# Other places for side work between the matrix products of a four-layer graph network, and one swap in the order of its block products

## The chip, the cores and the metric

The kernel runs on one core of one Trainium2 chip. The metric is the device time of one execution in microseconds, the median of several runs. A profiled execution of the same kernel gives the trace that the views below are taken from; its span runs from the first to the last instruction of the core.

## The reference

There are 3327 nodes with 256 features each, and one symmetric matrix `adj` of 3327 x 3327, in float32. Each of four layers normalises x over its features, takes the positive part and adds its result to x:

```python
h = relu(layernorm(x));  x = x + adj @ (h @ W.T + b)                      # layer 0
h = relu(layernorm(x));  A1 = top_k(tanh(adj*adj) where adj > 0, 700)     # layer 1
                         x = x + relu(A1 @ (tanh(h @ Wp + bp) @ Wg) + bg)
h = relu(layernorm(x));  A2 = D^-1/2 (adj + I) D^-1/2                     # layer 2
                         x = x + relu(A2 @ (h @ W.T))
h = relu(layernorm(x))                                                    # layer 3
R = rows of (adj + I) divided by their sums;  Xf = Xa = h;  Z = 0
for n in (0, 1):
    A = top_p_attention(Xa)      # softmax((Xa W1' W2')(Xa W3')'), the largest to 0.9 of the mass
    Xf = R @ Xf;  Xa = A @ Xa;  Z += Xf @ U1[n].T + Xa @ U2[n].T
x = x + layernorm(h + Z)
```

Every layer is therefore a product of a 3327 x 3327 matrix with 256 columns; layer 3 has two of them (R and A) in each of two steps, and the second step's A depends on the first step's result.

## The kernel before

The nodes are padded to 27 tiles of 128 rows. Rows are worked on in pairs, m and m + 13 (H = 13 pairs, T = 27 tiles). A pair's block product, seen as 2 x 2 blocks, is done with seven products of half size instead of eight: sums of blocks of `adj` (s1, s2, s4 and one in place, made by VectorE in `Feed.adding`, L553 to L556) and sums of the right side (`ts`). All of TensorE's work is float32 transposes and matmuls.

**Layers 0 to 2.** `products` loops over the pairs p = 0 to 12. `Product.steps` yields a number for each matmul call, called a step here; there are 7 x 13 = 91 for a pair, in three column cuts (`CUTS`, of 5, 4 and 4 blocks). In each cut the seven products come in the order of `PLACE`: 1, 2, 5, 4, 7, 3, 6. Product 5 uses s1 and product 3 uses s4, so that in the first cut s1 is first read at step 10 and s4 at step 25. When a product is finished (`result`, L619 to L630, and a `finish` function), the pair becomes a `Pair` of the next layer, which is normalised by VectorE (L404, and L460 for the last layer) and has a list of stages that TensorE must do: `turn` (transposes, L416, evicted by ScalarE at L420), `hidden` (L478, layer 1 only, followed by a tanh) and a last one: `second` (layer 1), `scaled` (layer 2) or `keys` (layer 3). The stages of pair p are put between the steps of the product of pair p + 1: the tables `WHERE`, `WHERE_KEYS` and `WHERE_FIRST` give the step numbers by how many stages there are. In layer 0 the first two pairs run together (`begin`), so that pair 2 carries the stages of two pairs, six in all. In layers 1 and 2 the first cut of the product of pair 1 is done early, inside that of pair 0 (`early`), and pair 0's stages are hooked into products 1 and 2 by a line of their own (`hooks, carried`). In layer 2 `counted` adds a small matmul (`pc`, L734) that sums the number of positive entries of a row pair over the partitions; its sum comes from VectorE (L724 to L729), and `counts` is read at the end of the kernel.

**Layer 3, first step.** `propagate_first` does R's product in 26 runs: pair p has two phases, each with products of 13 matmuls, in the order of `PHASES` (`FIRST_PHASES` for pair 0). `PLACE3` gives the accumulator bank of every product: 1, 2, 4 and 5 go to bank 0, 6, 7 and 3 to bank 1. After phase 0 (for pair 0 after phase 1) `half` copies bank 0 to SBUF on ScalarE (L1302), and there are two such accumulator buffers (`ps_acc`). A slab of 13 blocks of `adj` or of its stored sums is loaded through SP's queue when its product begins, and POOL adds the unit matrix to some (L1262). Between its matmuls the run does the attention of other rows: logits (L1061, four chunks: 0, 1 and 3 in `ps_row`, two buffers; 2 in both buffers of `ps_tr`), their exponentials on ScalarE (L1086), a threshold search (`search_steps`: one pass Relu at L1119 and one Sign at L1124 on ScalarE, the others on VectorE, ending with L1164 which keeps the large entries of e), and then the product of row m (`Rows`: transposes L202, evictions L205, matmuls L213). A finished row becomes, by `AttentionOfFirstStep`, a node of the second step: `turn`, `node` (L269 in one buffer of `ps_row`, evicted by L277 and L281, with a DMA L282) and `values` (L1344, also in `ps_row`). In the 19 interleaved rows these stand at fixed places of the run, which are in 27ths of its length: turn 3, node 9, logits of row m + 3 at 10, values 18, and the first transposes of row m + 1 at 20.

**Layer 3, second step.** The same search with the new keys; its first row (i = 0) also holds the last `turn` and `sums` of the first step's propagation (`of_next`).

TensorE's order is the program's: layer 3 is under a manual schedule in which TensorE keeps its order and the queues of the other engines are filled by a scheduler, with `high_priority` for evictions. [...] Several buffers are pairs, so that a matmul can wait for an eviction two uses before.

Of the kernel before, what the change touches and what calls it, by code (L numbers as in the profile page):

```python
# [47 lines left out]
def kernel(  # L48
# [94 lines left out]
    def run(steps, at=None):  # L143

        for k in steps:
            for what in (at or {}).get(k, ()):
                what()

    def merged(*plans):
        out = {}  # L150
        for p in plans:
            for k, v in p.items():
                out.setdefault(k, []).extend(v)
        return out
# [137 lines left out]
    def layers_0_to_2(again):  # L292
# [79 lines left out]
        def combine_nodes(rhs, a, b):  # L372
            run(combining_nodes(rhs, a, b))
# [258 lines left out]

        WHERE = {2: (60, 84), 3: (48, 61, 76), 6: (12, 22, 34, 46, 58, 70)}
        WHERE_KEYS = (81, 90)
        WHERE_FIRST = {2: (58, 86), 3: (52, 66, 83)}

        def products(layer, width, rhs, feed, finish, before, pair_after, following=None, counted=None, begin=None):

            todo = before.stages if before else []
            n, early = 0, []
            for p in range(H):
                if begin and p < 2:
                    if p == 0:
                        n, firsts = begin(lambda p: Product(layer, p, rhs, feed, width))
                    prod = firsts[p]
                else:  # L650
                    prod = early[0] if early and p == 1 else Product(layer, p, rhs, feed, width)
                    if p == 0:
                        for c in range(len(CUTS) if not before else 0):
                            combine_nodes(rhs, *CUTS[c])
                        if before:
                            combine_nodes(rhs, CUTS[2][0], H - 1)
                    at = WHERE_KEYS if layer == 2 and p else (WHERE if p else WHERE_FIRST).get(len(todo), ())
                    hooks = dict(zip(at, todo))
                    if early and p == 1:
                        hooks, carried = {86: todo[0]}, {14: todo[1]}  # L660
                    elif early and p == 2:
                        hooks.update(carried)
                    if counted:
                        hooks[62] = functools.partial(counted, p)

                    def steps(prod, c, a, b, past=0):
                        for at in prod.steps(c, a, b):
                            if at + past in hooks:
                                hooks[at + past]()

                    for c, (a, b) in enumerate(CUTS):
                        if early and p == 1 and not c:
                            n += 1
                            continue
                        feed.upto(n)
                        if p == 0 and before and b == H:
                            steps(prod, c, a, b - 1)
                            early.append(Product(layer, 1, rhs, feed, width))
                            steps(early[0], 0, *CUTS[0], 12 * 7)
                            combine_nodes(rhs, b - 1, b)  # L680
                            steps(prod, c, b - 1, b, 1000)
                        else:
                            steps(prod, c, a, b)
                        n += 1
                        if p == H - 1 and c and following:
                            combine_nodes(following, *CUTS[c - 1])
                    feed.upto(n)
                hold[:] = []
                if early and p == 0:
                    feed.upto(n + 1)  # L690
                    hold.append(feed.added)
                y, p3 = prod.result(feed.added if begin and p == 0 else None)
                x2 = feed.x2.pop(p)
                with tc.high_priority() if p == H - 1 else nullcontext():
                    finish(p, x2, y, p3)
                    pair = pair_after(p, x2)
                todo = pair.stages if p or not begin else []
                if begin and p == 1:
                    todo = first.stages + todo
                first = pair  # L700
            return pair
# [215 lines left out]
        else:  # L917
# [10 lines left out]
            with tc.tile_pool(name="tk", bufs=2) as tk, tc.tile_pool(name="tk1", bufs=1) as tk1:  # L928
# [9 lines left out]
                for p in range(H):  # L938
                    y = work.tile([P, 2, D], F32, tag="y", name=f"y1b_{p}")
                    for i in range(2):  # L940
                        m = p + i * H
# [54 lines left out]
    def layer_3_in(again, tag, big, ep, w3, sm3, h3, kT0, ksum0, left):  # L996
# [225 lines left out]

        added = []
        PHASES = (1, 2, 5, 4), (6, 7, 3)
        FIRST_PHASES = (1, 2, 3), (5, 7, 6, 4)
        PLACE3 = {2: (0, 0), 1: (0, 1), 4: (0, 2), 5: (0, 3), 6: (1, 0), 7: (1, 1), 3: (1, 2)}

        def combining(h, ts, a, b):
# [12 lines left out]
        class PropagatedPair:  # L1241
# [28 lines left out]
            def steps(self, phase):  # L1270

                first = self.p == 0
                ns = (FIRST_PHASES if first else PHASES)[phase]
                units = [(n, k) for n in ns for k in range(H)]
# [329 lines left out]
        with tc.manual_schedule(engines=PE_ALONE):  # L1604
# [10 lines left out]
            def passes(finder):  # L1615


                if finder is None:
                    return {}
                next(finder)  # L1620

                def one_more():
                    with tc.issue_after(last_turned[-1].ins):
                        next(finder, None)

                return {0: [one_more], 2: [one_more], 3: [lambda: next(finder, None)]}

            def passes_apart(step, finder):


                if finder is None:
                    return {}, {}

                first = passes(finder)[0]

                def second():
                    with tc.issue_after((last_copied if step == 0 else last_scaled)[-1].ins):
                        next(finder, None)
                    next(finder, None)

                return {0: first}, {4 if step == 0 else 0: [second]}
# [3 lines left out]
            def propagate_first(n, at):  # L1645

                p, phase = divmod(n, 2)
                pair = pairs.setdefault(p, PropagatedPair(0, p, h3, ts))
                units = H * len((PHASES if p else FIRST_PHASES)[phase])
                run(pair.steps(phase), {int(k * units // T): v for k, v in at.items()})  # L1650
# [42 lines left out]
            for i in range(EARLY):  # L1693
                plan = {}
                if props:
                    p = props.pop(0)
# [20 lines left out]
            rows = Rows(0, h3)  # L1717
# [3 lines left out]
            for m in range(T):  # L1721
                interleaved = m + AHEAD < T and m not in APART
                plan, later = passes_apart(0, finder) if interleaved else (passes(finder), {})
                plan = merged(plan, left_over)
                if props:
                    p = props.pop(0)
                    at = (3, 5, 6) if m == 0 else (2 if interleaved else 1, 3, 5)
                    plan = merged(plan, dict(zip(at, ([p.scale], [p.turn], [p.sums]))))
                if m + AHEAD < T and not interleaved:
                    plan = merged(plan, {4: [lambda: next(prepare(0, m + AHEAD, kT0))]})  # L1730
                alone = not interleaved and m != T - 3 and m + 1 < T
                if alone:
                    plan = merged(plan, {5: [lambda: rows.begin(m + 1)]})
                a = AttentionOfFirstStep(m, rows.finish(m, plan), dens.pop(m), f"{m}")
                if interleaved:
                    left_over = {}
                    steps = prepare(0, m + AHEAD, kT0)
                    after = {3: [a.turn], 9: [a.node], 18: [a.values], 20: [lambda: rows.begin(m + 1)]}
                    propagate_first(next(propagated), merged(whole_run(steps, 10), after, later))
                elif m == T - 3:  # L1740
                    left_over = {}
                    after = {1: [a.turn], 4: [a.node], 8: [a.values], 22: [lambda: rows.begin(m + 1)]}
                    propagate_first(T - LATE, after)
                elif alone:
                    left_over = {0: [a.turn], 1: [a.node], 3: [a.values]}
                finder = find(0, m + AHEAD, st0) if m + AHEAD < T else None
# [45 lines left out]
        with tc.manual_schedule(engines=PE_ALONE):  # L1792
# [3 lines left out]
            p = props.pop(0)  # L1796
            propagate_first(T - 2, merged(whole_run(steps_of_second, 8), {9: [lambda: p.scale(last_exp)], 16: [p.turn], 20: [p.sums]}))
            p = props.pop(0)
# [21 lines left out]
            rows = Rows(1, vs)  # L1820
# [3 lines left out]
            for i, m in enumerate(ORDER):  # L1824
                ahead = ORDER[i + AHEAD] if i + AHEAD < T else None
                plan, later = passes_apart(1, finder) if ahead else (passes(finder), {})
                if i == 0:
                    p, q = props
                    plan = merged({4: plan[0]}, {5: [p.scale, q.scale]})
                    of_next = {2: [p.turn], 5: [q.turn], 10: [p.sums], 14: [q.sums]}  # L1830
                acc = rows.finish(m, plan)
                ys[m] = attention_of_second_step(m, acc, dens.pop(m), f"{m}")
                plan = whole_run(prepare(1, ahead, kT1), 7) if ahead else {}
# [18 lines left out]
                p, phase = m % H, m // H  # L1852
# [111 lines left out]
```

## Time and profile before

| What | us |
|---|---|
| Median of 3 runs (lowest, highest) | 2517.3 (2516.82, 2521.48) |
| Profiled execution | 2517.92 |
| Its span | 2516.1 |
| TensorE busy, weight loads busy | 2486.4, 2254.9 |
| VectorE busy | 2095.5 |
| ScalarE busy | 1086.3 |
| POOL busy | 296.9 |

The mean clock that was granted to TensorE is 0.997 of full speed. PE are TensorE's matmuls, PEld its weight loads, DVE is VectorE, ACT ScalarE, POOL GpSimd and SP the engine that issues most transfers. A float32 matmul shows as two records. In a row of the timeline there stand start, duration, engine, line, operation, output and inputs, shape and number of records, and in brackets the idle time before it and the engine and line that ended it. A view of waits sums these brackets by the waiting line and the one waited for. The timeline puts neighbouring records of one line in one row, so a row's duration is from its first start to its last end.

### The profile page before, as it was taken

What the parts mean: (1) busy time and instruction counts of PE and PEld (TensorE: products, weight loads), DVE (VectorE), ACT (ScalarE), POOL (GpSimd) and SP (SyncE); (2) the same over time, 40 slices, a digit from 0 to 9 for tenths busy, and PEclk for the clock granted to TensorE, in tenths of its full rate; (3) what the DMA queues carried; (4) which work ended last, traced back from release to release, by engine and by line L of the source; (5) the groups of instructions that cost most, each with busy time, mean ns of one, the idle gap of its engine ahead of it and who ended that gap; (6) DMA issues with size and microseconds to landing.
All of it is one profiled execution on the core that took longest, in us unless ns stands there. A gap on an engine that the chain in (4) does not pass through costs nothing. (4 is left out here: it accounts for less than half of the span.)

```text
span 2516.1 us, 47844 instructions
## 1 busy us (share of the span) xinstructions
PE 2486.4 (99%) x17967; PEld 2254.9 (90%) x17967; DVE 2095.5 (83%) x5536; ACT 1086.3 (43%) x2158; POOL 296.9 (12%) x462
## 2 busy tenths in 40 slices
PE   9999999999999999999999999999999999999998
PEld 8999999999999998888888888888888888888887
DVE  7777788888887778788879797884999999999995
ACT  3011033443111115565656565663655655555551
POOL 2000010000000001000000100000121122222221
PEclk9999999999999999999999999999999999999999
DMA  6777765555698867223132323133533343344333
GB/s 200 226 227 240 224 196 172 177 174 182 224 311 299 275 213 233 96 81 108 57 112 88 108 85 105 55 108 104 172 118 112 108 138 119 109 134 141 117 117 105
DMA packets 181774, 388.28 MB, mean 154 GB/s; under 512 B 19741, under 2 KB 78746, under 8 KB 181530
## 3 DMA queue, kind: packets, MB, share of 16 engines
q1 hardware_dynamic: 153210, 364.31, 44.4%
q10 hardware_dynamic: 28320, 20.80, 2.6%
q8 instruction: 143, 2.34, 0.4%
q14 instruction: 101, 0.83, 0.1%
HBM read 315.44 MB, written 67.89 MB: 152 GB/s over the span
## 5 line engine op out<-in xcount | busy, mean ns | idle before, releaser
L205 ACT COPY eT_a<-pt_a 128x512 f32<-128x512 f32 (+1 forms) x364 | 196.7, 555 | 375.9 <-PE pt_a L202 372.6
L213 PE MATMUL a<-h3a,eT_a 128*128 128x256 f32 x1352 | 322.5, 381 | 0.2 <-ACT eT_a L205 0.2
L213 PE MATMUL a<-vs,eT_a 128*128 128x256 f32 x1352 | 320.2, 381 | 0.2 <-ACT eT_a L205 0.2
L1148 DVE MAX8 cand_a<-w 128x8 f32<-128x128 f32 x1352 | 288.4, 278 | 4.3
L213 PEld LDWEIGHTS a<-h3a,eT_a 128*128 128x128 f32 x1352 | 244.0, 189 | 32.8 <-issue 1.9
L213 PEld LDWEIGHTS a<-vs,eT_a 128*128 128x128 f32 x1352 | 244.8, 190 | 30.3 <-ACT eT_a L205 0.7
L603 PE MATMUL acc_a<-tsa,s_a 128*128 128x128 f32 (+1 forms) x2028 | 269.9, 275 | 0.0
L603 PE MATMUL acc_a<-tsa,a_a 128*128 128x128 f32 x2028 | 251.2, 275 | 0.0
L603 PE MATMUL acc_a<-rhs,a_a 128*128 128x128 f32 (+1 forms) x2028 | 250.3, 277 | 0.0
L603 PEld LDWEIGHTS acc_a<-tsa,s_a 128*128 128x128 f32 x2028 | 249.1, 192 | 0.6
L603 PEld LDWEIGHTS acc_a<-tsa,a_a 128*128 128x128 f32 x2028 | 239.5, 192 | 0.6
L603 PEld LDWEIGHTS acc_a<-rhs,a_a 128*128 128x128 f32 x2028 | 238.6, 193 | 0.6
L1144 DVE SCALAR_TENSOR_TENSOR w<-e_a,t_a 128x896 f32<-128x896 f32 x208 | 226.1, 1087 | 3.0
L1262 POOL TENSOR_TENSOR slab3a<-slab3a,ident 128x128 f32<-128x128 f32 x100 | 115.0, 1150 | 900.1 <-DMA slab3a<-in_adj_t_dram 383.7
L1086 ACT ACTIVATE e_a<-pl_a 128x1024 f32<-128x1024 f32 x260 | 184.7, 728 | 42.2 <-PE pl_a L1061 28.4
L202 PE MATMUL pt_a<-ident,e_a 128*128 128x128 f32 x1352 | 198.7, 273 | 0.6 <-DVE e_a L1164 0.3
L1135 DVE SCALAR_TENSOR_TENSOR w<-e_a,t_a 128x3328 uint8<-128x3328 f32 x52 | 191.8, 3689 | 4.3
L1164 DVE SCALAR_TENSOR_TENSOR e_a<-e_a,all_least 128x3328 f32<-128x3328 f32 x52 | 192.1, 3695 | 1.8
L202 PEld LDWEIGHTS pt_a<-ident,e_a 128*128 128x128 f32 x1352 | 165.5, 141 | 29.9 <-ACT eT_a L205 2.6
L420 ACT ACTIVATE xT_a<-pt_a 128x512 f32<-128x512 f32 x52 | 30.9, 595 | 355.7 <-PE pt_a L416 321.4
L753 ACT ACTIVATE a_a<-a_a 128x640 f32<-128x640 f32 (+1 forms) x156 | 101.5, 666 | 161.7 <-DVE a_a L751 129.1
L1293 PE MATMUL f0a<-tsa,slab3a 128*128 128x128 f32 x1352 | 166.2, 276 | 0.0
(265 smaller groups left out, 4213.0 us busy)
## 6 DMA issues: line engine op xcount, KB each, us to landing
slab3a<-s_dram SPq DMA_DIRECT2D x100, 832.0 KB, 4.4
a_a<-in_adj_t_dram SPq DMA_DIRECT2D x312, 256.0 KB, 4.0
slab3a<-in_adj_t_dram SPq DMA_DIRECT2D x79, 832.0 KB, 4.5
a_a<-in_adj_t_dram SPq DMA_DIRECT2D x156, 320.0 KB, 3.8
s_dram<-s_a SPq DMA_DIRECT2D x78, 256.0 KB, 4.9
s_dram<-s_a SPq DMA_DIRECT2D x39, 320.0 KB, 4.3
x_dram<-x_a ACTq DMA_DIRECT2D x39, 256.0 KB, 4.1
s_dram<-a_a SPq DMA_DIRECT2D x26, 256.0 KB, 5.1
```

Of the source, the lines that this page charges most:

```text
L202: nc.tensor.transpose(pt[:, j, :], e[:, k * P : (k + 1) * P], ident)
L205: last_turned.append(nc.scalar.copy(eT[:, : len(blocks), :], pt[:, : len(blocks), :]))
L213: nc.tensor.matmul(acc[:, :width], ready[g][:, j, :], rhs[:, k, :], start=(k == 0), stop=(k == T - 1))
L603: nc.tensor.matmul(self.acc[:, g, at : at + wide], quads[n][:, k - CUTS[c][0], :], t, start=(k == 0 and n in (1, 4)), stop=(k == H - 1 and ...
L753: nc.scalar.activation(a, a, AF.Tanh)
L1086: last_exp.append(nc.scalar.activation(dst, src, AF.Exp, accum_out=parts[:, c : c + 1]))
L1135: nc.vector.scalar_tensor_tensor(junk, e, t, e, ALU.is_lt, ALU.mult, accum_out=got)
L1144: nc.vector.scalar_tensor_tensor(w[:, : (b - a) * P], eg, t, eg, ALU.is_lt, ALU.mult, accum_out=below[:, g : g + 1])
L1148: nc.vector.max(cand[:, 8 * k : 8 * k + 8], w[:, (k - a) * P : (k - a + 1) * P])
L1164: nc.vector.scalar_tensor_tensor(e, e, least, e, ALU.is_ge, ALU.mult, accum_out=st["kept"][:, m : m + 1])
L1262: added.append(nc.gpsimd.tensor_tensor(x[:, p, :], x[:, p, :], ident, ALU.add))
L1293: nc.tensor.matmul(self.accs[bank][:, c * P : (c + 1) * P], a, self.right(n, k), start=start, stop=last.get(bank) == (n, k), skip_group_ch ...
```

## The change

There are six edits, all of them to places and orders; no operation is added or removed.

1. Layer 0: the six stages in pair 2 stand at steps 20, 30, 40, 50, 60, 72 instead of 12, 22, 34, 46, 58, 70.
2. Layer 1: in pair 0's product, which holds the last pair of layer 0, the stages `hidden` and `second` stand at 70 and 84 instead of 66 and 83.
3. Layers 1 and 2: pair 0's `turn` moves from step 86 of product 1 to step 10 of product 2, and its next stage from 14 to 34 there. The text of the change calls it the second pair's, since it stood in the second pair's product.
4. Layer 2: the count of pair 1 moves from step 62 of product 1 to step 22 of product 2; those of other pairs stay at 62.
5. Layer 3: in the second phase of pair 0 product 4 comes ahead of product 6, with its slab's load.
6. Layer 3: in the interleaved rows `node` moves from 9 to 15, and so behind the logits at 10; and in the first row of the second step the four items of `of_next` move from 2, 5, 10, 14 to 4, 8, 11, 15.

```diff
-        WHERE = {2: (60, 84), 3: (48, 61, 76), 6: (12, 22, 34, 46, 58, 70)}
+        WHERE = {2: (60, 84), 3: (48, 61, 76), 6: (20, 30, 40, 50, 60, 72)}
         WHERE_KEYS = (81, 90)
-        WHERE_FIRST = {2: (58, 86), 3: (52, 66, 83)}
+        WHERE_FIRST = {2: (58, 86), 3: (52, 70, 84)}
...
                     if early and p == 1:
-                        hooks, carried = {86: todo[0]}, {14: todo[1]}
+                        hooks, carried = {}, {10: todo[0], 34: todo[1]}
                     elif early and p == 2:
                         hooks.update(carried)
-                    if counted:
+                    if counted and early and p == 1:
+                        carried[22] = functools.partial(counted, p)
+                    elif counted:
                         hooks[62] = functools.partial(counted, p)
...
         PHASES = (1, 2, 5, 4), (6, 7, 3)
-        FIRST_PHASES = (1, 2, 3), (5, 7, 6, 4)
+        FIRST_PHASES = (1, 2, 3), (5, 7, 4, 6)
...
-                    after = {3: [a.turn], 9: [a.node], 18: [a.values], 20: [lambda: rows.begin(m + 1)]}
+                    after = {3: [a.turn], 15: [a.node], 18: [a.values], 20: [lambda: rows.begin(m + 1)]}
...
-                    of_next = {2: [p.turn], 5: [q.turn], 10: [p.sums], 14: [q.sums]}
+                    of_next = {4: [p.turn], 8: [q.turn], 11: [p.sums], 15: [q.sums]}
```

## The prediction

> **What bounds the kernel now.** I read the busy shares first, then TensorE's waits, then the timeline around each wait that the change touches. The chain that ended last shows only the kernel's tail (0% for every line), so it says nothing here.
>
> ```profile
> PE 2486.4 (99%) x17967; PEld 2254.9 (90%) x17967; DVE 2095.5 (83%) x5536; ACT 1086.3 (43%) x2158; POOL 296.9 (12%) x462
> ```
>
> TensorE is the bound: only what it idles, or runs at half clock, can be won. Its waits (releaser: us in total, times, longest):
>
> ```profile
> PE pt_a L416 <- DVE xn_a L404: 5.4, 4, 2.1
> PE pt_a L416 <- DVE h3a L460: 2.9, 1, 2.9
> PE f0a L1293 <- ACT xf_0a L1302: 2.4, 1, 2.4
> ...
> PE pc L734 <- DVE pos L729: 1.5, 1, 1.5
> PE pl_a L1061 <- ACT qT L281: 1.3, 4, 0.3
> PE hid_a L478 <- ACT xT_a L420: 0.8, 1, 0.8
> ```
>
> These six are what the change aims at. Around them in the timeline of TensorE and VectorE (start, duration, engine, line; the bracket is the idle time before):
>
> ```profile
> 84.68 0.76 PE L416 MATMUL pt_a<-ident,xn_a 128*128 128x128 f32 x4 [1.45 <-DVE xn_a L404]
> ...
> 400.77 1.11 PE L416 MATMUL pt_a<-ident,xn_a 128*128 128x128 f32 x4 [2.09 <-DVE xn_a L404]
> 401.68 1.91 PE L603 MATMUL acc_a<-tsa,s_a 128*128 128x128 f32 x8
> ...
> 401.56 0.82 DVE L553 TENSOR_TENSOR s_a<-a_a,a_a 128x640 f32<-128x640 f32 x1
> ...
> 691.27 0.18 PE L734 MATMUL pc<-ones,pos 128*128 128x1 bf16 x1 [1.49 <-DVE pos L729]
> ...
> 699.36 0.42 DVE L460 TENSOR_SCALAR h3a<-h3a 128x512 f32<-128x512 f32 x1
> 699.84 0.66 PE L416 MATMUL pt_a<-ident,h3a 128*128 128x128 f32 x4 [2.92 <-DVE h3a L460]
> ...
> 701.28 3.96 PE L603 MATMUL acc_a<-rhs,a_a 128*128 128x128 f32 x20
> ...
> 971.51 1.83 PE L1293 MATMUL f0a<-h3a,slab3a 128*128 128x128 f32 x14 [2.41 <-ACT xf_0a L1302]
> ...
> 998.09 3.67 DVE L1164 SCALAR_TENSOR_TENSOR e_a<-e_a,all_least 128x3328 f32<-128x3328 f32 x1
> ...
> 1002.21 1.04 PE L202 MATMUL pt_a<-ident,e_a 128*128 128x128 f32 x8
> ...
> 1437.07 1.13 PE L1061 MATMUL pl_a<-kT_0a,qT 64*128 64x512 f32 x4
> 1438.54 2.27 PE L1061 MATMUL pl_a<-kT_0a,qT 64*128 64x512 f32 x12 [0.34 <-ACT qT L281]
> ```
>
> ```profile
> 967.86:1001.77 33.91, 31.50 (x243) 27.58 (x242) 33.51 (x90) 22.70 (x48) 6.79 (x8) 1.00 0.61 206
> ```
>
> Undisturbed, 128-wide matmul records start every 0.112 us and a product step (two records) takes 0.223 us; 20 records of L603 take 2.40 us. The row at 701.28 takes 3.96: the clock granted after the two longest waits was half for 3.41 us, costing some 1.7 us each time, though the column reads 0.997 over the span. The last row gives, for 33.9 us, the busy time of PE, PEld, DVE, ACT and POOL: VectorE is full (33.51) just before e_0 is finished by L1164.
>
> [...] waits of 2.25 and 3.08 us by start times set it off, those of 1.66 and 2.57 didn't. [...] the eviction of qT (L281, 1438.23) stands behind the 3.07 us Sign pass (L1124) issued before it.
>
> **The change part by part.** Gains are TensorE's excess over its pace.
>
> *Layer 0, pair 2 holding two pairs' stages (WHERE[6]).* First turn 12→20, 8 steps = 1.78 us later. It waited 1.45 (1.61 with the restart), so it arrives 0.17 after its operand. The hidden stage follows 10 steps = 2.2 us after, the second another 2.2, against about 1.0 for the tanh between. Gain +1.65.
>
> *Layer 1, first pair (WHERE_FIRST).* Hidden 66→70: 0.89 us later against a wait of 0.80 (0.96 by starts). Second 83→84: the tanh ends at 375.08, arrival about 375.0. Gain +0.85, unless the next VectorE limit eats it.
>
> *Layer 1, pair 1's turn (step 86 of product 1) to step 10 of product 2, second stage from 14 to 34.* What goes: 2.25 of idle and 1.64 of half clock, 3.89. But product 2 now starts at about 398.6 instead of 403.4, and its operands come from a VectorE that is full there: s1 of L553 ends at 402.38, while the s1 steps begin at step 10, reached about 400.8. I allow that VectorE itself runs up to 0.85 earlier (its only wait there is a DMA): wait 0.7 to 1.6. Then s4 (L556), some fifteen steps on, about 1.0 more. Later slacks are 2.5 and over. The two layer-1 edits together: 4.75 less 2.2 of new waits, +2.5 (1.5 to 4.0). The stall goes from the transposes to the matmuls on s1 and s4; DVE L553 and L556 are late next.
>
> *Layer 2: pair 1's count from 62 of product 1 to 22 of product 2; its turn from 86 to 10, keys from 14 to 34.* The count's 1.73 and the turn's 3.08 + 1.66 go: 6.47. Product 2 starts about 695.9, its step 10 at about 698.4; h3 (L460) ends near 699.7 with four short sums of the result now ahead of it: a wait of about 1.3 stays[...]. Count at 62 of product 2 may wait 0.1 to 0.5. +4.7 (3.5 to 5.3). Its copy into counts is read only at the end.
>
> *First propagation, product 4 ahead of 6.* Bank 0 then finishes 13 units (2.9 us) earlier, so its eviction (L1302) no longer stands behind the 3.07 us Relu pass (L1119), and 2.57 at 971.5 goes. Slab 4 is loaded where slab 6 was: issued about 952.5, 4.5 us to land, then POOL's addition of the unit matrix (0.5 to 1.7), against a need at 959.9: covered by about 1 us, and not if the addition takes its slowest. But TensorE next needs e_0 at 1002.21, which L1164 delivers at 1001.76: the old slack is 0.45. VectorE's row above is full from 967.86, started by logits that this edit doesn't move, and two more MAX8 of 0.29 come before L1164. TensorE arrives at 999.6 and waits 2.4 to 3.0: the gain is handed back whole[...]. I take −1.5 (+0.4 to −2.3).
>
> *Keys (L269, L277, L281, DMA L282) from 9 to 15, behind the logits at 10, in 19 iterations.* The logits and the node's product share two PSUM buffers; before, the logits' second chunk waited for the node's eviction. Logits take 3.0 us undisturbed, 3.35 at five places, 3.67 at four: 5 × 0.35 + 4 × 0.67 = 4.4. Nothing is added: same matmuls, copies and DMA. In the new order the fourth chunk needs the exponential of the first, the node that of the second, the values (18) that of the fourth. With the Sign pass over at 1437.72, the exponentials (1.02, 1.01, 0.59, 0.60, 0.39 and their reads) run from there to about 1441.3; the node comes about 1441.5 and needs 1440, the values about 1442.4 and need 1441.3, the fourth chunk 1439.2 and needs 1438.8. The cover is 0.4 to 1.6 us; without it each costs what it lacks. ACT's own queue only has these copies later, as does qT's DMA, read in step 2. Gain +4.4 (2.5 to 4.8).
>
> *Second step's first row, {2,5,10,14}→{4,8,11,15}.* p's turn waits 0.56 at 1806.6, which goes; q's turn now comes behind the logits, which hold both transpose buffers until about 1813.3, against arrival at 1812.8. 0 (−0.5 to +0.5).
>
> Sum: 1.65 + 2.5 + 4.7 − 1.5 + 4.4 + 0 = 11.75. The profiled execution took 2517.92 (span 2516.1 and 1.8 around it), 0.6 over the median of 2517.3; taking the sum from the median gives 2505.5.
>
> **The rivals.**
> *A, the stalls go and nothing replaces them:* 1.77 + 1.03 + 3.89 + 6.47 + 0.45 + 4.4 + 0.5 = 18.5, 2499. For it: the waits are few and each is named. Against: VectorE's queue shows no room at 401 and 699.
> *B, VectorE is the bound wherever TensorE waits for it:* the layer 1 and 2 turns only move their stalls and again cross a half clock (+1 and +2.5), and half the logits' gain comes back at e_m or the copies. With layer 0 and −2 from the propagation: 1.65 + 1 + 2.5 + 2.2 − 2 = 5.3, 2512. For it: 33.51 busy of 33.91 before e_0; against: over 1060 to 1400 VectorE is busy 290 of 340.
> *C, slower:* in the 19 iterations the fourth chunk, behind the exponential of the first, takes the place of the second's wait, in every iteration and not in nine. Cover 0.4. All other parts give 7.35, and the logits' 4.4 might be had and paid back; it decides from (7.35 + 4.4)/19 = 0.62 us for each iteration, and at 0.9 gives 11.75 − 17.1 = −5.4, 2522.7. Against it: exponentials now wait for TensorE (28.4 of ScalarE's 42.2 idle before them), and the copies that stood before them are gone.
> *D, nothing moves:* VectorE paces layers and propagation alike and the logits' wait comes back in full, within 5.0 us: 2516. Against: stalls in layer 0 and in the nine logits have other causes.
>
> **How the numbers follow.** Likeliest forecast 0.50, A 0.17, B 0.18, D 0.08, C 0.07. About 0.2% (5.0 us) is what a measurement tells from no change. The forecast's own range, from the ends of layers 1, 2 and the keys, is 2501 to 2509. The range asked reaches into A and B: 2498.5 to 2512.5, leaving D, C and the outer edges. Faster 0.86 (forecast, A, B nearly whole), within 0.08, slower 0.06.
>
> **What would show it.** L416's waits near 84, 400 and 699 gone, smaller ones at L603 on s_a near 401 to 406, and at L416 on h3a of about 1.3; no half clock there. f0a's wait on L1302 gone, and a new one of 2.4 to 3.0 at L202 on e_a near 999, perhaps with 3.4 us of half clock. The logits at about 3.0 in all iterations and no wait on L281. Wrong would be: a wait over 2 us in product 2 of layer 1 or 2 with half clock; L1061, L269 or L1344 waiting for L1086 in most iterations; slab 4 late near 960.

## The result and the profile after

The changed kernel took 2506.75 us (median of 6 runs, 2505.51 to 2510.09) where the kernel before took 2518.11 (6 runs, 2516.82 to 2521.48). The ratio is 0.9954, with an interval of 0.9941 to 0.9967: faster, by 11.4 us in the medians. Timed once more beside it later, the ratio was 0.9969 (0.9958 to 0.9981). The forecast said 11.75. The total came out; its parts did not all, and that their errors cancelled is luck. The second timing gave 8.5.

TensorE's busy time and its waits in the changed kernel (line waiting, releaser: us in total, times, longest; lines after 660 stand two further down than before):

```profile
PE 2484.1 (99%) x17967; PEld 2256.5 (90%) x17967; DVE 2093.6 (84%) x5536; ACT 1085.2 (43%) x2158; POOL 298.4 (12%) x462
```

```profile
PE pt_a L202 <- DVE e_a L1166: 2.8, 2, 2.5
PE pt_a L416 <- DVE h3a L460: 2.2, 3, 1.1
...
PE pt_a L416 <- DVE xn_a L404: 1.3, 2, 0.7
PE pkq_a L269 <- DVE counts L738: 1.3, 2, 0.6
PE acc_a L603 <- DVE s_a L556: 0.7, 1, 0.7
```

The waits of f0a on L1302, of the count, of the hidden stage and of the logits are gone. Three are new: s4 (L556), which had been named as late next, e_0 before its transposes (L202 on L1166), also named, and one that nobody named: L416 on h3 three times in place of once, with L269 waiting for the count's copy. The timeline of TensorE and VectorE shows where:

```profile
403.36 1.38 PE L603 MATMUL acc_a<-rhs,s_a 128*128 128x128 f32 x10 [0.68 <-DVE s_a L556]
...
693.58 0.66 PE L416 MATMUL pt_a<-ident,h3a 128*128 128x128 f32 x4 [1.08 <-DVE h3a L460]
...
767.32 0.69 DVE L726 SCALAR_TENSOR_TENSOR pos<-a_a,pos 128x512 bf16<-128x512 f32 x1 [4.97 <-DMA a_a<-in_adj_t_dram]
...
776.89 0.66 PE L416 MATMUL pt_a<-ident,h3a 128*128 128x128 f32 x4 [0.40 <-DVE h3a L460]
...
781.02 0.71 PE L269 MATMUL pkq_a<-xT_a,kq 128*128 128x128 f32 x4 [0.63 <-DVE counts L738]
...
801.07 0.66 PE L416 MATMUL pt_a<-ident,h3a 128*128 128x128 f32 x4 [0.69 <-DVE h3a L460]
...
995.39 1.97 PE L202 MATMUL pt_a<-ident,e_a 128*128 128x128 f32 x8 [2.49 <-DVE e_a L1166]
...
1429.21 3.07 PE L1063 MATMUL pl_a<-kT_0a,qT 64*128 64x512 f32 x16
```

Near 777 and 801 we are in products 5 and 6 of layer 2, which the change doesn't touch. VectorE stood 4.97 us for a load of `adj` before the first and 4.36 and 1.42 before the second. What TensorE needs comes later in VectorE's rows: h3 (L460) at 776.42, 9.1 us behind the row that waited for the load, and the count's copy (L738, which TensorE's L269 waits for) at 780.82; between the load and h3 VectorE stands 1.14 us more, for POOL. The last row is the logits' block at the place shown before: one run of 16 records in 3.07 us.

To see what each step was worth, take the start of the same matmul (the n-th of its line) in both traces and subtract. The difference is TensorE's lead over the kernel before; what a stage adds to it is what the stage won. All leads below are against the first trace of the kernel before.

| Stage (us in the trace before) | Predicted | Lead grows | from, to |
|---|---|---|---|
| Before the change's first place | 0 | +0.42 | 0, 0.42 |
| Layer 0's stages (to 340) | +1.65 | +1.78 | 0.42, 2.20 |
| Layer 1 (to 666) | +2.5 | +3.8 | 2.20, 5.99 |
| Layer 2, to the end of product 2 (725) | +4.7 | +5.1 | 5.99, 11.12 |
| Layer 2, products 3 to 12 (921) | 0 | −4.3 | 11.12, 6.80 |
| First propagation and first transposes (1052) | −1.5 | −1.05 | 6.80, 5.75 |
| Keys behind the logits (1737) | +4.4 | +3.5 | 5.75, 9.29 |
| Second step's first row (1873) | 0 | −0.3 | 9.29, 9.01 |

TensorE thus ends 9.05 us earlier. The spans differ by 10.97; the other 1.92 lie behind TensorE's last matmul (11.26 us to the end before, 9.34 after), where nothing was changed. In the fourteen traces of all kernels this tail was 9.2 to 11.3 us: 11.26 and 11.03 in the kernel before, 9.34 to 9.83 in the changed one, and 10.88 in a kernel that differs from it only by the node's place. Why it differs was not tested.

### The profile page after: what moved, and what is told of

Read it like the earlier page. It is cut to its first block, busy times and chain, and to the rows that moved or that the text cites. A ratio compares the mean times of both kernels' runs of the same rounds, so it can differ in the third digit from the quotient of the medians.

```text
span 2505.2 us, 47792 instructions
## 1 busy us (share of the span) xinstructions
PE 2484.1 (99%) x17967; PEld 2256.5 (90%) x17967; DVE 2093.6 (84%) x5536; ACT 1085.2 (43%) x2158; POOL 298.4 (12%) x462
## 5 line engine op out<-in xcount | busy, mean ns | idle before, releaser
L603 PE MATMUL acc_a<-tsa,s_a 128*128 128x128 f32 (+1 forms) x2028 | 269.9, 275 | 0.0
L603 PE MATMUL acc_a<-tsa,a_a 128*128 128x128 f32 x2028 | 251.6, 275 | 0.0
L603 PEld LDWEIGHTS acc_a<-tsa,s_a 128*128 128x128 f32 x2028 | 248.8, 192 | 0.7
L603 PE MATMUL acc_a<-rhs,a_a 128*128 128x128 f32 (+1 forms) x2028 | 248.6, 276 | 0.0
L603 PEld LDWEIGHTS acc_a<-tsa,a_a 128*128 128x128 f32 x2028 | 239.6, 192 | 0.5
L603 PEld LDWEIGHTS acc_a<-rhs,a_a 128*128 128x128 f32 x2028 | 236.7, 192 | 0.6
L202 PE MATMUL pt_a<-ident,e_a 128*128 128x128 f32 x1352 | 199.7, 274 | 3.0 <-DVE e_a L1166 2.8
L1088 ACT ACTIVATE e_a<-pl_a 128x1024 f32<-128x1024 f32 x260 | 184.5, 728 | 36.9 <-PE pl_a L1063 35.4
L202 PEld LDWEIGHTS pt_a<-ident,e_a 128*128 128x128 f32 x1352 | 166.2, 141 | 32.4 <-DVE e_a L1166 2.7
L1166 DVE SCALAR_TENSOR_TENSOR e_a<-e_a,all_least 128x3328 f32<-128x3328 f32 x52 | 191.9, 3690 | 1.8
```

What stands on the lines that cost most here:

```text
L202: nc.tensor.transpose(pt[:, j, :], e[:, k * P : (k + 1) * P], ident)
L603: nc.tensor.matmul(self.acc[:, g, at : at + wide], quads[n][:, k - CUTS[c][0], :], t, start=(k == 0 and n in (1, 4)), stop=(k == H - 1 and ...
L1088: last_exp.append(nc.scalar.activation(dst, src, AF.Exp, accum_out=parts[:, c : c + 1]))
L1166: nc.vector.scalar_tensor_tensor(e, e, least, e, ALU.is_ge, ALU.mult, accum_out=st["kept"][:, m : m + 1])
```

## The experiments

The three open questions were: what takes 4.3 us back in layer 2; what the swap of products 4 and 6 is worth; and whether layer 1's and the logits' terms are the edits' own. The leads of all traces, in us, at the end of layer 1 (666), of layer 2's product 2 (725), of layer 2 (921), 60 us after the first row's transposes (1066), at the end of the first step (1738), and at TensorE's end:

| Kernel | 666 | 725 | 921 | 1066 | 1738 | end |
|---|---|---|---|---|---|---|
| changed | 5.99 | 11.12 | 6.80 | 6.10 | 9.29 | 9.05 |
| changed, second trace | 5.93 | 11.06 | 8.55 | 7.59 | 10.73 | 10.20 |
| changed, third trace | 5.72 | 8.30 | 6.21 | 5.40 | 8.56 | 8.27 |
| layer 2 as before | 5.41 | 5.63 | 5.63 | 4.29 | 7.44 | 7.15 |
| layer 1 as before | 5.28 | 9.12 | 7.96 | 7.09 | 10.25 | 9.95 |
| product 6 first | 6.37 | 8.79 | 8.33 | 7.08 | 10.26 | 9.99 |
| keys at 9 | 5.87 | 10.47 | 8.55 | 6.85 | 6.90 | 6.64 |
| turn at 20 | 6.63 | 11.95 | 9.90 | 8.55 | 11.73 | 11.47 |
| slabs later | 3.65 | 8.21 | 8.08 | 6.73 | 9.89 | 9.62 |
| centre first | 5.43 | 8.06 | 7.97 | 9.66 | 12.83 | 12.54 |
| together | 7.16 | 12.81 | 12.07 | 13.76 | 16.92 | 16.61 |
| together, second trace | 6.25 | 12.17 | 11.81 | 13.51 | 16.70 | 16.36 |
| before, second trace | 0.85 | 0.11 | −0.31 | −1.97 | −1.94 | −1.91 |

**Layer 2 as before.**

```diff
                         hooks, carried = {}, {10: todo[0], 34: todo[1]}
+                        if layer == 2:
+                            hooks, carried = {86: todo[0]}, {14: todo[1]}
...
-                    if counted and early and p == 1:
+                    if False:
```

> The changed kernel with layer 2's edits undone: the count of pair 1 at step 62 of product 1, the first pair's turn at 86 and its keys at 14 of product 2. Theory (transfers set the pace of layer 2): the waits of 1.7 and 3 us and the half clock come back at products 1 and 2 (5.1 us), but the two pairs of waits of the changed kernel in products 5 and 6 (4.3 us) go, because TensorE no longer runs ahead of the loads. TensorE's gain over the kernel before at the end of layer 2 stays within 1.5 us of the changed kernel's 6.8, and the time is 0 to 1.5 us above the changed kernel's. Rival (the waits in products 5 and 6 have nothing to do with how early product 2 starts): they stay, the gain at the end of layer 2 is 6.8 - 5.1 = 1.7, and the time is some 5 us above the changed kernel's.

It took 2509.06 us (ratio 0.9974, 0.9964 to 0.9984), 2.3 over the changed kernel by the medians, a little more than expected; this interval meets those of the changed kernel (0.9941 to 0.9967, 0.9958 to 0.9981), so the traces must decide. The waits came back at their old places, and from 760 to 830 us TensorE waited for nothing:

```profile
685.85 0.18 PE L738 MATMUL pc<-ones,pos 128*128 128x1 bf16 x1 [1.47 <-DVE pos L733]
...
694.47 1.12 PE L416 MATMUL pt_a<-ident,h3a 128*128 128x128 f32 x4 [2.98 <-DVE h3a L460]
```

The lead at the end of layer 2 is 5.63, 1.2 under the changed kernel's first trace. Within layer 2 this kernel gained 0.2; the eight traces that have the changed kernel's orders and slabs there, with its turn at 10 or at 20, gained 0.5 to 3.3, 2.1 on the mean (from the table, 921 less 666). So layer 2's edits, worth 5.1 at product 2, were worth some 2 at the layer's end.

**Slabs later.** The first slabs of layer 3 (three of 832 KB) may be loaded only behind the loads of a given pair of layer 2: pair 4 before and after the change. In the changed kernel two of them are issued at 739.3 and 740.1, the third at 756.3, between loads of `adj`.

```diff
-                    if self.layer == 2 and p == 4:
+                    if self.layer == 2 and p == 8:
```

> The changed kernel with the first three slabs of layer 3 allowed behind the loads of pair 8 of layer 2 in place of pair 4. Theory (the three slabs of 832 KB, put between the loads of pairs 4 to 6, make the loads late, and VectorE and then TensorE wait): the waits at the turn, the keys and s4 in products 5 and 6 go; TensorE's gain over the kernel before at the end of layer 2 rises from 6.8 to between 9 and 11, and the time falls by 2 to 4.3 us against the changed kernel. Rival (the loads are late without the slabs): the waits stay in products 5 and 6, the gain stays at 6.8. A third way: the waits only move to products 9 and 10, with the same sum.

2506.08 us (0.9954, 0.9937 to 0.9971), not the 2 to 4.3 us faster that were expected. The waits in products 5 and 6 are gone, but this trace had lost 2.6 us in layer 1, whose code is the same, and came to product 3 with a lead of only 8.21, of which it kept 8.08. Another trace with the slabs behind pair 4, centre first below, kept 7.97 of 8.06. So the lead alone does not tell the two apart. The loads do. The four loads of `adj` that are issued just behind the third slab took 8.0 to 8.9 us to land in the changed kernel's first trace, and 6.3 to 9.7 in the eight traces with slabs behind pair 4's loads and the turn at 10 or 20. The same four loads, counted in order of issue, took 5.3 to 5.8 here and 4.7 to 6.5 in the two traces of "together" below, where no slab is near. In the eight traces VectorE then stood 3.7 to 5.7 us for one load near 767; in the three with later slabs none of its rows that start between 761 and 776 had waited for a load (in the first trace of "together" the row at 776.64 waited 3.34).

**Turn at 20.** More lead, with the slabs as they were:

```diff
                         hooks, carried = {}, {10: todo[0], 34: todo[1]}
+                        if layer == 2:
+                            carried = {20: todo[0], 40: todo[1]}
```

> The changed kernel with layer 2's first turn at step 20 of product 2 in place of 10, and its keys at 40 in place of 34. Theory: the wait of 1.3 to 2.4 us of the turn on h3 goes (10 steps are 2.2 us), and the gain after product 2 rises by as much; with the slabs still behind pair 4's loads, waits in products 5 and 6 take most of it back, so that the gain at the end of layer 2 stays between 6.8 and 8.6, as in the three traces with the same layer 2 so far (6.8, 8.3, 8.6). Rival (nothing is taken back): 9 to 10.5.

2506.23 us (0.9954, 0.9937 to 0.9970). The wait on h3 went; in its place the matmuls on s4 wait 0.8. Of 11.95 us of lead, 2.05 were taken back in products 5 and 6, less than was expected: 9.90 falls to the rival's range, though the waits that the rival denies were there. TensorE's waits in this kernel from 680 to 830 us (those of L269 in products 5 and 6, that of L603 in product 2):

```profile
PE pkq_a L269 <- DVE counts L740: 1.1, 2, 0.6
PE acc_a L603 <- DVE s_a L556: 0.8, 1, 0.8
```

**Product 6 first.**

```diff
-        FIRST_PHASES = (1, 2, 3), (5, 7, 4, 6)
+        FIRST_PHASES = (1, 2, 3), (5, 7, 6, 4)
```

> The changed kernel with product 6 ahead of product 4 again in the second phase of pair 0. Theory (VectorE's chain to the first row's e sets the start of the row's transposes): the wait of 2.4 us for the copy of bank 0 comes back, the wait of 2.5 us before the transposes goes, and so does the half clock behind it; TensorE's gain at those transposes stays at 6.8 within 0.5, and 60 us later it is 0.5 to 1.1 us above the changed kernel's; the time is the same to 1.1 us faster. Rival (the swap is worth its 2.6 us): 2.6 us slower than the changed kernel.

2505.92 us (0.9958, 0.9944 to 0.9972): the same time. The 2.4 us for the copy of bank 0 are back, those before the transposes gone:

```profile
963.17 2.73 PE L1295 MATMUL f0a<-h3a,slab3a 128*128 128x128 f32 x14 [2.40 <-ACT xf_0a L1304]
...
995.48 0.71 PE L202 MATMUL pt_a<-ident,e_a 128*128 128x128 f32 x5
```

Either way one wait of about 2.6 us (by start times) stands in this stretch; the swap only moves it. I had expected this order to spare the half clock, and it did not: here it fell behind the copy (granted clock 0.83 from 962 to 972), in the changed kernel behind e_0. From 921 to 1066 the changed kernel lost 0.7 to 1.0 in its three traces, and 0.9 to 1.35 in four other kernels with its order and its logits (layer 1 and layer 2 as before, slabs later, turn at 20); this one lost 1.25, and the second trace of the kernel before 1.7 against its first. The swap's own worth is not told from nothing.

**Keys at 9.**

```diff
-                    after = {3: [a.turn], 15: [a.node], 18: [a.values], 20: [lambda: rows.begin(m + 1)]}
+                    after = {3: [a.turn], 9: [a.node], 18: [a.values], 20: [lambda: rows.begin(m + 1)]}
```

> The changed kernel with the node at 9 again, ahead of the logits. Theory: the logits take 3.35 and 3.67 us again at nine places, and eight small waits of 0.1 us of the row's first products on their evictions, which the later copies caused, go: TensorE gains 3.5 us less between the first row's transposes and the end of the first step. Rival (the reorder's own gain is the whole 4.4 and something else took 0.9 us): 4.4 us less.

2510.95 us (0.9977, 0.9969 to 0.9985). The logits wait again:

```profile
1431.67 2.27 PE L1063 MATMUL pl_a<-kT_0a,qT 64*128 64x512 f32 x12 [0.34 <-ACT qT L281]
```

From 1066 to 1738 it gained 0.05, the changed kernel 3.14 to 3.19 in its three traces: the steadiest number of the study. With the first of the nine places, which lies ahead of 1066, that is the 3.5 of the table. The nine cost 4.4 (five of 0.35, four of 0.67). The changed kernel gives 1.0 of it back: at eight rows from 1416 on, a first product on an eviction starts 0.12 us later than here, because the eviction comes only at the end of the 3.07 us of the Relu pass on ScalarE. At the place shown below that pass begins 0.61 us after the eviction ahead of it, here 0.48; why it begins later was not tested. In the changed kernel:

```profile
1443.46 3.07 ACT L1121 ACTIVATE junk_a<-e_a,t_a 128x3328 uint8<-128x3328 f32 x1
...
1446.53 0.57 ACT L205 COPY eT_a<-pt_a 128x512 f32<-128x512 f32 x1
```

**Layer 1 as before.**

```diff
                         hooks, carried = {}, {10: todo[0], 34: todo[1]}
+                        if layer == 1:
+                            hooks, carried = {86: todo[0]}, {14: todo[1]}
...
-        WHERE_FIRST = {2: (58, 86), 3: (52, 70, 84)}
+        WHERE_FIRST = {2: (58, 86), 3: (52, 66, 83)}
```

> The changed kernel with layer 1's edits undone (hidden and second at 66 and 83; the first pair's turn at 86 of product 1, the second stage at 14 of product 2). Theory: the waits of 0.8 and 2.1 us come back with the half clock; TensorE's gain over the kernel before after layer 1's product 2 is 3.8 us less than the changed kernel's (2.1 in place of 5.9), and as the transfers of layer 2 follow TensorE's start of that layer, most of it stays lost: 2.5 to 4.5 us slower than the changed kernel. Rival (layer 2's transfers take back whatever comes before them too, so that its end does not move): within 1 us of the changed kernel's gain at the end of layer 2.

2505.87 us (0.9947, 0.9927 to 0.9967): not slower, so the theory did not hold. Its lead at the end of layer 2, 7.96, lies 1.2 above the changed kernel's first trace and between its three (6.21 to 8.55). In time, then, layer 1's edits are not told from nothing. Behind product 2 of layer 1 its lead is 5.18 against 5.89. The wait was smaller and no half clock followed (granted clock 1.00 from 395 to 402):

```profile
397.11 0.76 PE L416 MATMUL pt_a<-ident,xn_a 128*128 128x128 f32 x4 [1.08 <-DVE xn_a L404]
```

In the kernel before, VectorE had waited 0.86 us for a load at 392.1, 8.2 us before its xn (L404); here it didn't.

**Before once more, changed once more.** To see how far a trace repeats:

> The kernel before once more, for a second trace of the same code. Theory: the count's wait of 1.7 us and the turn's of 3.1 us in layer 2 with its half clock, the copy's of 2.6 us and the logits' nine are the same; the turn's wait in layer 1's product 1 is the one that moves, 2.2 us with a half clock where VectorE has waited 0.9 us for a transfer just before, and about 1.2 us without a half clock where it has not. Rival: it is 2.2 us with a half clock again, and only the earlier layer 0 changed it in the run with layer 1 as before.

2519.66 us. At the turn in layer 1:

```profile
391.35 1.61 DVE L751 SCALAR_TENSOR_TENSOR a_a<-a_a 128x640 f32<-128x640 f32 x2 [1.15 <-DMA a_a<-in_adj_t_dram]
...
399.94 0.76 PE L416 MATMUL pt_a<-ident,xn_a 128*128 128x128 f32 x4 [2.39 <-DVE xn_a L404]
```

The wait is 0.3 longer, with VectorE's wait for the load 0.3 longer; and there was no half clock (1.00 from 399 to 405), so neither expectation held whole. In layer 2 the count waited 1.26 and the turn 4.29, not 1.66 and 3.08.

> The changed kernel once more, for a second trace of the same code. Theory: the gain after layer 2's product 2 lies between 8 and 12 us and the gain at the layer's end between 6.8 and 8.6, the further ahead the more is taken back in products 5 and 6; before the first row's transposes a wait of 2.6 us, with 0.7 to 1.7 us of half clock behind it; between there and the end of the first step +3.2 within 0.1. Rival: the end of layer 2 moves one to one with the gain after product 2.

> The changed kernel once more, timed beside the kernel with the three further edits. Theory: 9 to 12.5 us under the kernel before; its trace has the waits in products 5 and 6 of layer 2 if its gain after product 2 is over 9 us.

2506.39 us and 2508.14 us (0.9969, 0.9958 to 0.9981; 8.5 under the kernel before in the medians, a little less than expected). The second and third traces lost 2.5 and 2.1 in products 5 and 6, the third from a lead of 8.30 only: the size of the lead alone does not set what is taken back. In the third, VectorE waited 1.02 us for a load ahead of h3, and the turn in product 2 waited 2.01, twice the 1.08 of the first trace, with half clock behind it (0.83 from 690 to 700):

```profile
688.40 0.49 DVE L724 TENSOR_SCALAR pos<-a_a 128x640 bf16<-128x640 f32 x1 [1.02 <-DMA a_a<-in_adj_t_dram]
...
694.77 0.66 PE L416 MATMUL pt_a<-ident,h3a 128*128 128x128 f32 x4 [2.01 <-DVE h3a L460]
```

**Centre first.** If VectorE's chain from the first row's logits sets the transposes, the logits must come earlier. Before, VectorE's fourth sum (2.03 us) stood ahead of the centring that the logits need.

```diff
-        FIRST_PHASES = (1, 2, 3), (5, 7, 4, 6)
+        FIRST_PHASES = (1, 2, 3), (5, 7, 6, 4)
...
+                    last_centred[:] = [nc.vector.tensor_scalar(k, k, mean[r : r + DA, :], None, ALU.add)]
...
+                    def fourth_sum():
+                        with tc.issue_after(last_centred[-1].ins):
+                            next(sums_of_first)
-                    centred = {7.5: [lambda: centre(kT0, mean0(), "0"), lambda: next(sums_of_first)]}
-                    propagate_first(1, merged(centred, whole_run(steps, 14.5), plan))
+                    centred = {5: [lambda: centre(kT0, mean0(), "0")], 9: [fourth_sum]}
+                    propagate_first(1, merged(centred, whole_run(steps, 11.5), plan))
```

> The changed kernel with product 6 ahead of 4 again, and the centring of the keys (TensorE's mean at 5 in place of 7.5, VectorE's fourth sum of 2.0 us behind the centring and not ahead of it) and the first row's logits (11.5 in place of 14.5) earlier. Theory (VectorE's chain from these logits sets when the first row's transposes start): e of the first row comes 1.5 to 2 us earlier, the wait for the copy of bank 0 shrinks to about 1 us, the wait before the transposes goes, and no half clock follows: TensorE's gain 60 us after them is 2.4 to 3.2 us above its gain at the end of layer 2 less 0.7 to 1.7, so 1.5 to 2 us above that at the end of layer 2. Rival (another operand sets the transposes): no gain beyond product_6_first, which lost 1.3 us there.

2504.33 us (0.9946, 0.9926 to 0.9965). From 921 to 1066 the lead grew by 1.7, where all other kernels with the later logits lost 0.7 to 1.7 against the first trace of the kernel before. The copy's wait is 1.1, and e_0 no longer makes TensorE wait:

```profile
962.21 1.83 PE L1297 MATMUL f0a<-h3a,slab3a 128*128 128x128 f32 x14 [1.07 <-ACT xf_0a L1306]
...
987.74 3.68 DVE L1168 SCALAR_TENSOR_TENSOR e_a<-e_a,all_least 128x3328 f32<-128x3328 f32 x1
...
992.91 1.04 PE L202 MATMUL pt_a<-ident,e_a 128*128 128x128 f32 x8
```

Product 6 stands ahead of 4 as in the run with product 6 first; what differs is the centring and the logits. VectorE's last step to e_0 (L1168) starts at 987.74 here, and there (L1166) at 990.02. So it is VectorE's chain from these logits that set the transposes.

**Together.** Slabs later, turn at 20 and centre first at once, twice.

> The three edits at once on the changed kernel: the slabs behind pair 8's loads, layer 2's turn at 20 and keys at 40, and the centring and logits earlier with product 6 ahead of 4. Theory: with the slabs out of the way layer 2 keeps what the turn wins: its own gain is 5.5 to 7 us (4.4 with the slabs later alone), and the first step's start adds 1.5 to 2: 2500 to 2502 us, 4 to 7 faster than the changed kernel. Rival (layer 2's loads set its end with or without the slabs): its own gain stays at or under 4.4 and the time is 2503 or more.

> The three further edits at once, once more, for an interval. Theory: 14 to 17 us under the kernel before and 4 to 6.5 under the changed kernel; layer 2 keeps at least 11 us of gain to its end, with at most one wait near products 9 and 10. Rival (the first trace was lucky in layer 2): a gain at the end of layer 2 under 9.

2501.92 us (0.9938, 0.9918 to 0.9958), and 2499.76 us (0.9934, 0.9921 to 0.9948), the latter 8.4 under the changed kernel timed beside it, more than expected: the intervals don't meet. Layer 2's own gain was 4.91 and 5.56, under the 5.5 to 7 expected in one of the two. With a lead of 12.8 and 12.2 after product 2, products 5 and 6 took nothing back. 0.7 and 0.4 went near 890; whether the slabs, now issued from 822 on, did that stays open, since product 6 first lost 0.5 at the same place with early slabs. Turn at 20, alike in layer 2 but for the slabs, lost 2.05 from 11.95 in products 5 and 6. So did every trace with pair 4's slabs that came there with more than 9 us of lead: five of five, 1.2 to 4.3. With the landing times above (6.3 to 9.7 us against 4.7 to 6.5) this shows the cause: the slab loads among those of pairs 4 to 6. Over all traces with pair 4's slabs and the changed or the later turn, products 3 to 12 took back 0.1 to 4.3, mean 1.8 (eight traces); with pair 8's, 0.1 to 0.7, mean 0.4 (three).

## Why the prediction was right, and where it was not

*Layer 0.* As forecast: 1.78 for 1.65; the wait of 1.45 at 84.68 is gone (the turn at 84.42 waits for nothing).

*Layer 1.* The mechanism held in half: the stall went to the matmuls on s4 (0.68 at 403.36, about 1.0 forecast), but the one forecast on s1 (0.7 to 1.6) stayed out: L553 ended at 398.57, 3.8 us earlier than before and not the 0.85 at most that I allowed, just ahead of its first use at 398.73. The rows of the changed kernel:

```profile
397.75 0.82 DVE L553 TENSOR_TENSOR s_a<-a_a,a_a 128x640 f32<-128x640 f32 x1
...
398.73 0.39 PE L603 MATMUL acc_a<-tsa,s_a 128*128 128x128 f32 x2
```

The size, +2.5, is between what was seen: +3.8 against the first trace of before, +2.1 behind product 2 against its second trace, but only 0.7 against the kernel with layer 1 undone. The term that was mis-sized is what goes, 3.89: its 1.64 of half clock was absent both in before's second trace and in the kernel with layer 1 undone (1.00 from 399 to 405 and from 395 to 402), and its 2.25 was 2.56 in the one and 1.24 in the other, where VectorE had stood 1.15 and 0 for the load in place of 0.86.

*Layer 2.* At product 2 as forecast: +5.1 for +4.7, with the wait of about 1.3 on h3 (1.08; 1.25 by starts) in its place. That no half clock would follow is right for that trace (1.00 from 690 to 700) and not for all: in four others the wait was 2.1 to 2.5 by starts, and in three of these half clock stood behind it (product 6 first, centre first and the third trace of the changed kernel, 0.83 from 690 to 700 in each). The step that failed is what stands after it: the forecast carried the 4.7 to the end without asking what paces the rest of the layer. Of it, 4.3 was taken back in products 5 and 6 (2.1 and 2.5 in the other traces), because VectorE there waits for loads (4.97 and 4.36 us) among which the slabs stand. No rival named this: B has TensorE wait for a VectorE that is full, and here VectorE itself stood 4.97 us for a load. What B says of product 2, a turn with half clock behind it again, and what the forecast lists as a sign of being wrong, did come in the three traces just named: in the changed kernel's third trace layer 2's edits won 2.6 by the end of product 2 (5.72 to 8.30), B's 2.5.

*The first propagation.* As argued: 2.57 gone (the copy, L1304, now runs at 960.84, ahead of the Relu pass at 961.30), 2.65 before e_0 come, then half clock (granted clock 0.79 from 994 to 1002), which the forecast had as an estimate. −1.05 for −1.5; slab 4 was not late (TensorE waits for nothing from 936.93 to e_0). One reading in the forecast is off: it says that half clock followed the two longest waits. It followed the longest (3.08 by starts, 0.50 from 701.14) and the third (2.25, 0.50 from 400.77); the second, the 2.57 of this very place, had none (1.00 from 970 to 980).

*The logits.* +3.5 for 4.4. The nine waits went; the cover was there (no wait of L1063, of the node's pkq or of L1346 is in the list), but evictions of the row behind the Relu pass of 3.07 us, which the forecast did not count, cost 0.12 at eight rows. Rival C, slower, has no trace here.

*The second step's first row.* −0.3, within its range and as argued: p's wait of 0.40 went, and q's turn now waits 0.46 for the exponentials of the logits (L162 on L1088 at 1803.63). The logits themselves took 0.23 longer there.

The sum held by luck: layer 1's excess (+1.3), the tail's 1.92 and the start's 0.42, none of them forecast, made up for most of layer 2's 4.3 and the logits' 0.9. The forecast's own range is 2503 to 2510 by the ends it names; its 2501 also takes the propagation's upper end. One trace of this kernel, whose lead at the end of layer 2 was 6.80, 8.55 and 6.21 in three, does not carry terms to half a microsecond.

## What to carry to other kernels

When a stall is taken away early in a stage, ask what paces the rest of that stage: here, of the 11.12 us of lead that TensorE had won, 4.3 went back where VectorE stood 4.97 us for one load and a prefetch for the next stage was among the loads; with the prefetch later 0.1 to 0.7 went back. A wait was moved here, not removed, by reordering the waiting engine (2.41 us for the copy before, 2.49 for e_0 after), where VectorE, which the later one ended on, was busy 33.51 of 33.91 us; what helped was to follow that engine's chain to its first input and to move that. Before a wait of one trace is booked as gain, see whether the releasing engine had itself been held by a transfer just before, and take a second trace.

## What the runs showed that was not expected

Idle time and half clock: nearly the same wait had half clock behind it in one trace and not in another. At the turn in layer 1 an idle of 2.25 us by starts (2.09 as a wait) in before's first trace had it (granted clock 0.50 from 400.77 to 404.18), one of 2.56 (2.39) in its second trace did not (1.00 from 399 to 405). At the copy of bank 0 the 2.57 (2.41) of before's first trace did not (1.00 from 970 to 980), and a wait of 2.5 in its second did (0.81 from 971 to 980). The wait of 2.5 before e_0's transposes had it in the changed kernel's first and second traces (0.79 from 994 to 1002 and from 992 to 1000), and so had the 2.40 for the copy with product 6 first (0.83 from 962 to 972). So between 2.0 and 2.6 us the length of a wait does not tell, in these traces, whether half clock stands behind it; what does was not shown.

Behind the three waits that have it in the first traces of the two kernels the granted clock is 0.50 for 3.41 us each time (from 400.77 and 701.14 before, from 994.94 after). The 20 records of L603 from 701.28 take 3.96 us there and 2.40 elsewhere, so one and the same code can come out some 1.6 us apart at one wait.

And traces of one code differed by 2.3 us at layer 2's end (6.80, 8.55, 6.21), though by 0.5 at most in the tail.
